# Four-layer transformer on one core: x kept in SBUF between the second layer's cross attention and its GEGLU, and the context loaded 10 slots ahead

## The chip, the core and the metric

The kernel runs on one core of a Trainium2 chip. The metric is device time in microseconds (us): the median of three runs before the change is 4973.1 us (4965.27 to 4977.62). One further execution was profiled; every view below is of that one. The engines are TensorE (PE; its weight loads are PEld), VectorE (DVE), ScalarE (ACT), GpSimd (POOL) and SyncE (SP). Each works through its own queue strictly in order. SP computes nothing: it issues the DMA transfers, and an issue at the head of its queue that has to wait holds up all behind it.

## What is computed

The input is `x`, 32 batches of 112 x 256 numbers, and a context of 32 batches of 375 x 256. Four layers follow each other; the second one is what matters here (`ln` is a layer norm, `fq` rounds to 8 bits and clips):

```python
# layer 1 (counted from 0), cut
x = attn(ln1(x), ln1(x)) + x                 # sweep l1s: self attention
x = attn(ln2(x), context) + x                # sweep l1x: cross attention, 16 heads, quantised
hg = ln3(x) @ ff_w1 + ff_b1                  # sweep l1f: GEGLU
a, g = split(hg, 2)
x = a * gelu(g) @ ff_w2 + ff_b2 + x

def attn(h, ctx):                            # 16 heads of width 16
    sim = fq(h @ wq) . fq(ctx @ wk) * scale
    out = fq(softmax(sim), dw, 0) . fq(ctx @ wv)
    return out @ wo + bo
```

Layers 0, 2 and 3 are a cross attention (l0x), a cross attention with a feed-forward (l2x, l2f), and self attention, cross attention and feed-forward (l3s, l3x, l3f). The context is the same array each time.

## The kernel before

**Sweeps, units, slots.** Each of the nine sweeps goes over all 32 batches. Two sweeps may run beside each other (`PAIRS`, L29): l1x, and with a delay l1f, are such a pair. A sweep is a list of units. A unit of l1x (`unit16`, L1005) is one batch and has 8 slots, one for each pair of heads; a unit of l1f (`unitff`, L1218) is two batches and 8 slots. `order` (L1333) merges the slots of both sweeps into one sequence by a made-up time, in which l1f runs some seven batches behind l1x.

**Work ahead of a slot.** Beside its slots a unit has atoms: pieces of work with a lead (`LEAD`, L79), the number of slots of its own sweep by which each stands ahead of the unit's first slot; a negative lead stands behind it. Atoms with cost 0 are put out when due; the others are spread as filler between slots by `fill` (L1468). `run` (L1363) writes everything out in that order, and the framework's scheduler then sets the final order of each engine's queue from a timeline of its own, and hands out the buffers. A tile names a tag; a tag has a fixed number of buffers (`BUFS`, L64), and a new tile waits until one is free.

**One pair of heads in l1x** goes through these lines: scores on PE (L1106), row maximum on DVE (L606), a small scaling on ACT (L609), the exponential on ACT (L612) into a tile of tag `k3`, times the quantisation step on ACT (L641), reciprocal on DVE (L646), scale and round on POOL or DVE (L213), clip to bf16 on DVE (L657) into another `k3` tile whose padding POOL clears (L1117). After two pairs a DMA issued by SP transposes four heads' probabilities (L1125, `k3` to `k3`), and PE multiplies them with the values (L1070). So a batch has four such transposes; I count them 0 to 3 within the batch.

**Context.** `ctx_atoms` (L530) loads one batch's context already transposed by the host (L541, 375 KB, into `k3`, then named `k<-in_ctxT_dram`), 14 slots ahead (`cload=14`). At the same lead (`cut=14`) the high part is copied into a tile of tag `k6` on ACT and DVE in turn (L200 or L202, share `("l1x", "ctx"): (1, 1, 0)`), POOL subtracts to get the low part (L231), and both are stored to DRAM (L552, `cd<-k`, 752 KB) for the later layers. The key projection on PE reads the `k6` tile first, 4 slots ahead.

**Values for layer 2.** `values_atoms` (L488) computes, as filler in l1x, four blocks a batch of layer 2's values: PE (L235 to L237), copies on ACT (first two thirds) and DVE (last third) into one `k3` tile, and a store of 375 KB (L502, `vd<-k`, 125 partitions x 3,072 bytes). So each transpose on SP has one such store near it.

**x.** In `load_x` and `store_x` (L380, L388), a sweep whose successor runs beside it can leave x in SBUF (`beside`, L373). l1x and l1f are excepted by `AGAIN` (L378): l1x loads x (lead 17) for its norm, lets the buffer go, loads x again 7 slots into the unit (`again=-7`) for the residual (L1206), and stores the sum to DRAM; l1f does the same from there (`again=-3`, residual at L832). Tag `x` has 11 buffers of 1 KB a partition, tag `k6` has 5 of 6,016 bytes.

Of the kernel before, what the change touches and what calls it, by code (L numbers as in the profile page):

```python
# [8 lines left out]
F32 = mybir.dt.float32  # L9
# [8 lines left out]
S = 112  # L18
# [3 lines left out]
D = 256  # L22
# [6 lines left out]
PAIRS = [("l0x", "l1s"), ("l1x", "l1f"), ("l2x",), ("l2f", "l3s"), ("l3x", "l3f")]  # L29
# [28 lines left out]
def mm_cost(n, m, passes):  # L58
    return passes * max(n, 2 * m) / 2.4


class Kern:
# [7 lines left out]
        l1x=[0, 1, 3, 6, 7],  # L70
        l1f=[0, 1, 5, 0, 3],
# [7 lines left out]
    LEAD = dict(  # L79
        l0x=dict(load=11, stats=10, apply=6, cload=11, cstats=8, cut=8, ctrans=5, q=4, k=[2, -2], v=-1),  # L80
        l1s=dict(load=5, stats=5, apply=3, q=2, k=2, v=1),
        l1x=dict(load=17, stats=12, apply=10, cload=14, cut=14, q=8, apart=[2, -1], k=4, v=-1, v2=[-2, -4, -6, -7], again=-7),
        l1f=dict(load=13, stats=11, apply=10, gate=2, gelu=1, again=-3),
        l2x=dict(load=10, stats=7, apply=6, cload=11, cut=7, q=4, k=[1, 1], v=0, vload=2),
        l2f=dict(load=6, stats=5, apply=3),
        l3s=dict(load=10, stats=8, apply=7, q=7, qload=3, k=6, v=3, c2=4, k2=1, v2=1),
# [285 lines left out]

    def beside(self, i):  # L373

        return any(self.sweeps[i : i + 2] == list(p) for p in PAIRS) and self.sweeps[i] not in self.AGAIN


    AGAIN = ("l1x", "l1f")  # L378

    def load_x(self, s, b):  # L380
        i = self.sweeps.index(s)
        if i and self.beside(i - 1):
            return self.xd[i - 1, b]
        x = self.t([S, D], F32, "x")
        self.nc.sync.dma_start(x, self.A["x"][b] if i == 0 else self.xd[i - 1, b])
        return x

# [440 lines left out]

    def residual(self, s, b0, g):

        for e, x in enumerate(g["xr" if s in self.AGAIN else "x"]):
            self.nc.vector.tensor_tensor(x, g["acc"][:, e, :], x, ALU.add)  # L832
            self.store_x(s, b0 + e, x)

# [170 lines left out]
    def unit16(self, s, b0, i, gb, g, wd, quant, self_attn, qb, kb, vb, dl, gvec, bvec):  # L1005
# [3 lines left out]
        L = self.LEAD[s]  # L1009
        u = Unit()  # L1010
        st = {}
        both = int(quant and self_attn)
        apart = quant and not self_attn
# [14 lines left out]
        if not self_attn and not quant and self.early_kv():  # L1028
            b = b0 + i
# [167 lines left out]
        u.slots = [quad(qd) for qd in range(4)] if self_attn else [pair(pr) for pr in range(8)]  # L1197

        def fin():
            x = st["xr"] if s in self.AGAIN else g["x"][i]  # L1200
            po = self.ps([S, D])
            wo = wd["o"]
            self.bias_mm(s, po)
            for c in range(2):
                self.mm3(po, lambda q: st["ot"][:, q, c, :], lambda q: wo[:, c, q, :], False, c == 1)
            nc.vector.tensor_tensor(x, po, x, ALU.add)  # L1206
            self.store_x(s, b0 + i, x)

        u.slots[-1].st[4] = fin
        if s in self.AGAIN:  # L1210
            u.atoms.append((L["again"], 0, lambda: st.update(xr=self.load_x(s, b0 + i))))
        return u


# [3 lines left out]
    def unitff(self, s, b0, gb, wd, gvec, bvec, b1, glu):  # L1218
        nc = self.nc
        W = gb * S  # L1220
        L = self.LEAD[s]
        u = Unit()
        u.needs = [b0 + e for e in range(gb)]
        g = {}

        u.atoms += self.norm_atoms(s, b0, gb, g, gvec, bvec, raw=glu)

        def up(ch):
            pf = self.ps([128, W])
            if glu:  # L1230
                w = wd["1", ch // 8]
                for k in range(2):
                    nc.tensor.matmul(pf, w[:, k, (ch % 8) * 128 : (ch % 8) * 128 + 128], g["h"][:, k, :], start=k == 0, stop=k == 1)  # L1233
                return pf
            w = wd["1", ch // 4]
            for k in range(2):
                self.mm3(pf, lambda i: w[:, k, i, (ch % 4) * 128 : (ch % 4) * 128 + 128], lambda i: g["h"](k, i), k == 0, k == 1)
            return pf

        def gate(c):  # L1240
            if c == 0:
                g["g"] = self.t([128, 8, W], F32, "qs")
            pf = up(c + 8)
            self.shift("gate", g["g"][:, c, :], pf, b1[:, c + 8 : c + 9])

        if glu:
            for c in range(8):
                u.atoms.append((L["gate"] + 7 - c, mm_cost(W, 0, 8), lambda c=c: gate(c)))

            u.atoms.append((L["gelu"], 0, lambda: nc.scalar.activation(g["g"], g["g"], AF.Gelu)))  # L1250

        def mk(c):
            z = {}

            def a():
                if c == 0:
                    g["acc"] = self.ps([S, gb, D], "acc")
                    self.bias_mm(s, g["acc"])
                pf = up(c)
                uu = self.t([128, W], F32, "s1")  # L1260
                if glu:
                    nc.vector.scalar_tensor_tensor(uu, pf, b1[:, c : c + 1], g["g"][:, c, :], ALU.add, ALU.mult)
                    z["uu"] = uu
                    return
                self.shift("relu", uu, pf, b1[:, c : c + 1], AF.Relu)
                ul = z["ul"] = self.t([128, 2, W], F32R, "ot")
                self.split(uu, ul[:, 0, :], ul[:, 1, :], ("upper", "lower"))

            def b():
                w = wd["2"] if glu else wd["2", c // 4]  # L1270
                for i in range(gb):
                    if glu:
                        nc.tensor.matmul(  # L1273
                            g["acc"][:, i, :], z["uu"][:, i * S : (i + 1) * S], w[:, c, :],
                            start=False, stop=c == 7 and i == gb - 1,
                        )
                        continue
                    self.mm3(
                        g["acc"][:, i, :], lambda q: z["ul"][:, q, i * S : (i + 1) * S], lambda q: w[:, c % 4, q, :],
                        False, c == 7 and i == gb - 1,  # L1280
                    )
                if c == 7:
                    self.residual(s, b0, g)

            return Slot(a, None, b)

        u.slots = [mk(c) for c in range(8)]
        if s in self.AGAIN:
            u.atoms.append((L["again"], 0, lambda: g.update(xr=[self.load_x(s, b0 + i) for i in range(gb)])))
        return u  # L1290


# [302 lines left out]
```

## Time and profile before

| | us | |
|---|---|---|
| median of three runs | 4973.1 | 4965.27 to 4977.62 |
| profiled execution | 4961.83 | its span 4960.0, so 1.8 lie around the span |
| PE busy | 4515.7 | 91% of the span |
| DVE busy | 3631.7 | 73% |
| ACT busy | 3417.2 | 69% |
| POOL busy | 2110.2 | 43% |
| l1x's score matmuls (L1106, bf16) | 1152.4 to 2309.5 | first and last start, from the span's start |

Busy time is the time in which an engine executes an instruction; waits are not in it. "PEclk" in the profile is the share of its full clock that TensorE was granted. A row of the waits names who waited, at which line and for which tile, then who ended the wait, then the total, the number and the longest. In a row of the timeline the bracket at the end is the engine's idle time just before, and what ended it.

### The profile page before, as it was taken

To read this page: it belongs to the slowest core of one execution; us is meant where nothing else is said; L and a number is where in the kernel's file an instruction comes from. 1 tells how busy PE (TensorE), PEld (TensorE's weight loads), DVE (VectorE), ACT (ScalarE), POOL (GpSimd) and SP (SyncE) were. 2 spreads that over 40 slices of the span, in tenths; PEclk is the share of its full clock that TensorE was granted. 3 is DMA by queue.
4 is the path that set the end of the run, shared out by engine and by line. 5 is a ranking of instruction groups with operands and counts; after the bars stand their busy time and mean duration, and the time that the engine had idled before them with its cause. 6 is when DMAs were issued, how large, how long until landed. Compare 5 with 4: busy or idle time off the path is not lost.

```text
span 4960.0 us, 111607 instructions
## 1 busy us (share of the span) xinstructions
PE 4515.7 (91%) x37824; PEld 4007.3 (81%) x37824; DVE 3631.7 (73%) x9806; ACT 3417.2 (69%) x10644; POOL 2110.2 (43%) x3674
## 2 busy tenths in 40 slices
PE   6999999998779888888999999998999986899999
PEld 5888888886668777777999999998888875788888
DVE  4788888888887777776688888886555554777776
ACT  4788888887777776675577777774555544677776
POOL 4455555555443333332233333334333332556655
PEclk9999999999889999999999999999999997999999
DMA  4433333335676666676454555443665666666662
GB/s 102 124 84 86 84 81 84 86 84 132 138 148 134 131 134 134 132 147 132 112 142 143 143 143 143 142 132 109 206 192 177 205 191 192 171 159 160 161 160 77
DMA packets 585414, 674.53 MB, mean 136 GB/s; under 512 B 318688, under 2 KB 495056, under 8 KB 584656
## 3 DMA queue, kind: packets, MB, share of 16 engines
q1 hardware_dynamic: 584848, 667.40, 53.3%
q8 instruction: 305, 5.00, 0.4%
q14 instruction: 261, 2.14, 0.1%
HBM read 323.55 MB, written 173.02 MB: 100 GB/s over the span
## 4 chain that ended last, share of the span: by engine, by line
PE 39%; DMA 7%; DVE 4%; ACT 1%; SPq 1%; issue 1%; POOL 1%; ACTq 0%; DVEq 0%; POOLq 0%
PE ps L664 6%; PE ps L235 5%; PE ps L236 4%; PE ps L237 4%; PE sc L773 3%; PE ps L795 3%; PE ps L1070 3%; DMA qs<-dq_l3s 2%; PE sc L1106 2%; PE acc L235 1%; PE acc L237 1%; DMA k<-cd 1%; PE acc L236 1%; PE ps L1233 1%; PE acc L1273 1%
## 5 line engine op out<-in xcount | busy, mean ns | idle before, releaser
L217 POOL TENSOR_SCALAR k<-k,sm 112x375 f32<-112x375 f32 (+1 forms) x1536 | 928.7, 617 | 1051.7 <-DVE sm L646 475.9
L200 ACT ACTIVATE k<-ps 125x336 f32<-125x336 f32 (+4 forms) x2005 | 912.4, 468 | 418.8 <-PE ps L237 194.9
L606 DVE TENSOR_REDUCE sm<-sc 112x1 f32<-112x375 f32 x1792 | 947.0, 540 | 177.0 <-PE sc L773 88.9
L612 ACT ACTIVATE k<-sc,sm 112x375 f32<-112x375 f32 x1536 | 878.2, 577 | 106.7 <-DVE sm L606 86.6
L664 PE MATMUL ps<-ident,k 112*125 112x112 f32 x4608 | 730.2, 276 | 17.4 <-issue 4.2
L664 PEld LDWEIGHTS ps<-ident,k 112*125 112x125 f32 x4608 | 649.0, 189 | 69.9 <-issue 36.3
L773 PE MATMUL sc<-k,qs 128*112 128x376 f32 x2048 | 540.9, 357 | 18.0 <-ACT k L612 9.0
L235 PE MATMUL ps<-w,k 128*125 128x256 f32 (+2 forms) x1344 | 433.4, 322 | 33.1 <-ACT k L612 17.5
L235 PE MATMUL ps<-h,w 128*128 128x224 f32 x1408 | 409.4, 297 | 42.5 <-DVE h L202 15.9
L695 DVE TENSOR_TENSOR k<-ps,k 64x376 fp32r<-64x376 f32 x640 | 350.1, 547 | 121.5 <-ACT k L200 106.2
L236 PE MATMUL ps<-h,w 128*128 128x224 f32 x1408 | 393.4, 282 | 0.5 <-DVE h L231 0.5
L202 DVE COPY k<-ps 125x336 f32<-125x336 f32 (+2 forms) x619 | 289.2, 467 | 141.2 <-PE ps L237 71.7
L237 PE MATMUL ps<-h,w 128*128 128x224 f32 x1408 | 391.5, 281 | 0.0
L236 PE MATMUL ps<-w,k 128*125 128x256 f32 (+2 forms) x1344 | 389.6, 290 | 0.0
L237 PE MATMUL ps<-w,k 128*125 128x256 f32 (+2 forms) x1344 | 388.9, 289 | 0.0
L235 PE MATMUL ps<-k,w 128*128 128x376 f32 x896 | 343.8, 384 | 41.6 <-DMA k<-cd 28.7
L213 POOL TENSOR_SCALAR k<-k,sm 112x375 f32<-112x375 f32 x256 | 164.4, 642 | 448.4 <-DVE sm L646 279.4
L795 PE MATMUL ps<-k,k 125*64 125x112 f32 (+1 forms) x4608 | 350.7, 296 | 2.1 <-ACT k L200 1.3
L773 PEld LDWEIGHTS sc<-k,qs 128*112 128x112 f32 x2048 | 304.8, 177 | 47.0 <-ACT k L612 23.6
L235 PEld LDWEIGHTS ps<-h,w 128*128 128x128 f32 x1408 | 272.3, 196 | 69.7 <-issue 20.2
L235 PEld LDWEIGHTS ps<-w,k 128*125 128x125 f32 (+2 forms) x1344 | 263.5, 196 | 73.6 <-ACT k L612 28.2
L612 ACT ACTIVATION_READ_ACCUMULATOR k<-sc,sm 112x1 f32 x1536 | 321.1, 209 | 0.0
(213 smaller groups left out, 12642.2 us busy)
## 6 DMA issues: line engine op xcount, KB each, us to landing
qs<-h SPq DMA_DIRECT2D x512, 224.0 KB
k<-k SPq DMA_DIRECT2D x192, 376.0 KB
k<-cd SPq DMA_DIRECT2D x64, 752.0 KB
vd<-k SPq DMA_DIRECT2D x128, 375.0 KB
k<-vd SPq DMA_DIRECT2D x128, 375.0 KB
qs<-dq_l3s SPq DMA_DIRECT2D x256, 112.0 KB
qs<-dq_l3x SPq DMA_DIRECT2D x256, 112.0 KB
x<-xd SPq DMA_DIRECT2D x224, 112.0 KB
```

Of the source, the lines that this page charges most:

```text
L200: self.nc.scalar.activation(out, in_, AF.Identity)
L202: self.nc.vector.tensor_copy(out, in_)
L217: self.nc.gpsimd.tensor_scalar(out, in_, by, 1.0, ALU.mult, ALU.mult)
L235: mm(out, lhs(0), rhs(0), start=start, stop=False)
L236: mm(out, lhs(0), rhs(1), start=False, stop=False)
L237: mm(out, lhs(1), rhs(0), start=False, stop=stop)
L606: nc.vector.tensor_reduce(nms[j], sc[j][:, :n], AX.X, ALU.max, negate=True)
L612: nc.scalar.activation(p[:, j, :n], sc[j][:, :n], AF.Exp, bias=nms[j], scale=1.0 if scale is None else scale, accum_out=sm[:, j : j + 1])
L664: self.nc.tensor.transpose(pst[:TB, a * S : (a + 1) * S], p[:, j, a * TB : (a + 1) * TB], self.ident[:S, :S])
L695: nc.vector.tensor_tensor(ks[o, j, :], pk[r, :TE], ks[r, j, :].bitcast(F32), ALU.subtract)
L773: nc.tensor.matmul(sc[:, :TE], qs[:, hd, q, bs], kk, start=q == 0, stop=q == 1)
L795: nc.tensor.matmul(o if gqa else o[:, mm, :], vq[:, a, hd * 64 : hd * 64 + 64], st["pt"][:, :, j, ta] if gqa else st["pt", mm][:, j, ta], ...
```

## The change

l1x and l1f no longer load x again, and l1x no longer stores x: what l1x leaves in SBUF is what l1f reads. Sixteen batches of x are held at a time: 11 in the tag `x`, and the first 5 of every 16 as slices of one tile that takes one of the five `k6` buffers from the first load of l1x until l1f's batch 20 is done. The context's load and cut move from 14 to 10 slots ahead.

```diff
-        l1x=dict(load=17, ..., cload=14, cut=14, ..., v2=[-2, -4, -6, -7], again=-7),
-        l1f=dict(load=13, stats=11, apply=10, gate=2, gelu=1, again=-3),
+        l1x=dict(load=17, ..., cload=10, cut=10, ..., v2=[-2, -4, -6, -7]),
+        l1f=dict(load=13, stats=11, apply=10, gate=2, gelu=1),
...
-        return any(self.sweeps[i : i + 2] == list(p) for p in PAIRS) and self.sweeps[i] not in self.AGAIN
-    AGAIN = ("l1x", "l1f")
+        return any(self.sweeps[i : i + 2] == list(p) for p in PAIRS)
+    ROUND, MORE = 16, 5
...
-        x = self.t([S, D], F32, "x")
+        n = b % self.ROUND
+        if s == "l1x" and n < self.MORE:
+            assert b < self.ROUND or (i + 1, b - self.ROUND) in self.xd
+            if b == 0:
+                self.more = self.t([S, self.MORE, D], F32, "k6")
+            x = self.more[:, n, :]
+        else:
+            x = self.t([S, D], F32, "x")
...
-        for e, x in enumerate(g["xr" if s in self.AGAIN else "x"]):
+        for e, x in enumerate(g["x"]):
...
-            x = st["xr"] if s in self.AGAIN else g["x"][i]
+            x = g["x"][i]
...
-        if s in self.AGAIN:
-            u.atoms.append((L["again"], 0, lambda: st.update(xr=self.load_x(s, b0 + i))))
...
-        if s in self.AGAIN:
-            u.atoms.append((L["again"], 0, lambda: g.update(xr=[self.load_x(s, b0 + i) for i in range(gb)])))
```

Lines from L385 on stand 7 further down in the changed kernel, from L1212 on 5, and from L1290 on 3. In the text both kernels' lines are named by their numbers before.

## The prediction

> **What bounds it now.** I read the header, then busy time by stretch, then the waits of the stretch that the edit touches, engine by engine, and last the timeline of one stall. By the page PE is the busiest engine:
>
> ```profile
> span 4960.0 us, 111607 instructions
> PE 4515.7 (91%) x37824; PEld 4007.3 (81%) x37824; DVE 3631.7 (73%) x9806; ACT 3417.2 (69%) x10644; POOL 2110.2 (43%) x3674
> ```
>
> The edit touches only l1x and l1f, 1150 to 2310 us. Stretches (duration, busy time and count of PE, PEld, DVE, ACT, POOL, then clock, DMA share, GB/s):
>
> ```profile
> 1000.00:1150.00 150.00, 142.89 (x1149) 120.83 (x1148) 126.50 (x366) 125.22 (x407) 81.40 (x153) 1.00 0.35 88
> 1150.00:1450.00 300.00, 231.66 (x1754) 190.55 (x1754) 266.66 (x718) 217.18 (x667) 138.24 (x252) 0.87 0.67 141
> 1450.00:2250.00 800.00, 693.71 (x5176) 614.27 (x5175) 603.96 (x1693) 564.83 (x1528) 289.25 (x444) 0.94 0.69 137
> ```
>
> Until 1450 DVE sets the pace (267 of 300 us); the edit gives it no work and takes none. From 1450 to 2250 PE is idle 106 of 800 us, and no engine is full. So that stage is bound by waits. PE's, ACT's and SP's:
>
> ```profile
> PE ps L1070 <- DMA k<-k: 64.0, 37, 5.6
> PE ps L443 <- ACT k L612: 23.1, 15, 2.5
> PE ps L235 <- ACT k L612: 9.3, 9, 2.2
> ```
>
> ```profile
> ACT k L612 <- DMA vd<-k: 22.7, 10, 4.2
> ```
>
> ```profile
> SPq L385 <- DMA xd<-x: 129.4, 42, 6.3
> SPq L502 <- DVE k L202: 129.1, 52, 8.4
> SPq L385 <- DVE xh L441: 98.7, 26, 9.1
> ```
>
> PE waits for the transposed probabilities (64 us) and for exponentials that give PSUM back. SP stands 228 us of 1160 before loads of x, which the edit removes. One stall shows the chain:
>
> ```profile
> 1637.06 0.93 SPq L541 DMA_DIRECT2D k<-in_ctxT_dram  x1
> 1639.50 0.27 SPq L502 DMA_DIRECT2D vd<-k  x1
> 1639.88 4.30 SPq L1125 DMA_TRANSPOSE k<-k  x1
> ...
> 1640.70 0.55 DVE L202 CAST k<-k 128x752 fp32r<-128x752 f32 x1 [0.35 <-DMA k<-in_ctxT_dram]
> ...
> 1647.20 0.66 ACT L612 ACTIVATE k<-ps,sm,sc 112x375 f32<-112x375 f32 x1 [4.24 <-DMA vd<-k]
> 1648.47 0.33 PE L1070 MATMUL ps<-k,k 128*32 128x112 bf16 x12 [3.66 <-DMA k<-k]
> ```
>
> The store of layer 2's values frees the buffer of the next exponential only 7 us after its issue; ACT loses 4.24 us and PE 3.66. A transpose right behind such a store takes 4.3 us to issue (42 issues within 0.3 us of one: median 4.28); from 3 us after it on, 1.5.
>
> **Removed.** 128 DMAs of 112 KB: 64 repeated loads, 32 stores by l1x, 32 first loads by l1f. Their place on the DMA engines: in 1800 to 1900 us the packets of 1,024 bytes take 90 us of 16 x 100, 6%; that lies beside other work, as the engines are busy 69%. Their SP time is what counts. I went through all 128 transposes, from the last clip (L657) to the issue: 240 us of that lateness is L385 and 50 us L396. But PE waits for 46 of them only, 79 us in all, nearly always transposes 1 and 3 of a batch, and these stand behind a value store, not behind x. Capped by PE's wait at each, the x issues cost PE 8 us. Another 20 us of lateness at the waiting ones is SP still issuing the transpose before, which x made late in part. I take **-12 us**, between -8 and -18.
>
> **Kept or added at nothing.** DVE, ACT and POOL do the same instructions on x in the same shapes. A load of x now waits for the store of the batch 16 before: in the built order 22 of 23 such loads follow that store by one to three places, some 16 pairs of waits of about 3 us (x stores landed 1.9 to 5.2 us after issue): 48 us of SP against 228. Behind it stand transposes with even number, for which PE rarely waits; uncovered it would cost those 48. With four `k6` buffers the next owner's key matmuls come at least 47 us of PE work after the last read of the old one (66 before): covered. (PE work is counted on its queue, each matmul at the 30th percentile of its form's interval from start to start, so without waits. The sum over the program is equal in both kernels, 3730 us.)
>
> **Moved: the context step.** Every batch's load, copy, subtraction and store go four slots later, 18 us at 1157 us for 256 slots, past one value store and one transpose on SP. From the load's release to the first key matmul PE had about 36 us of work, now 20. The way there: landing, copy 0.83, subtraction 1.8 with up to 2.5 of wait, some 14 us after release: covered by 5 us; if a batch used that up, PE would lose what is over.
>
> The wait that I price is the copy's. ACT and DVE reach it in order, and behind it stand the next pair's exponentials. In the built order of ACT in the changed kernel:
>
> ```
> L211 xh <- ps1
> L641, L609, L612, L612, L641
> L200 k6 <- k3        (the context's copy)
> L609, L612, L612     (next pair)
> ```
>
> Counting in PE work from the moment X at which the load may go, the instruction that feeds this copy is at X+5.5 to 6.5 before and at X+0.4 to 1.2 after, for 13 of ACT's 16 copies. After the change ACT gets there at 0.4 to 1.2 + 0.6 (L211) + 0.3 + 0.3 + 2 x 0.85 + 0.3, so about X+4.3. On SP the load now stands right behind a value store, whose last copy on DVE ends some 2 us after X: store issued at X+2.3, load at X+3.1. Alone a context load has its last packet 2.2 to 3.2 us after its issue, and is seen 0.3 later. But behind a value store? Of that the trace of before has no context load, but 13 loads of x issued within 0.7 us of one: their last packet came 3.5 to 5.8 us after issue, against a median of 1.3 for the others; value stores end 5.5 after issue. So the context lands between X+6 (unhindered) and X+8.7 (behind the store), and ACT waits 1.6 to 4.4 us. I take 4.2, the row with the same neighbour: 13 or 14 times 4.2 is 57 us of ACT.
>
> What of it reaches PE? At the ten waits of L612 for a value store (22.7 us) I summed PE's idle time during each and in the 6 us after: 26 us, of which 6 to 9 would be there anyway at 13% idle; a share of 0.75 to 1.1. I take 0.9: **+52 us** (ends: 16 from 1.6 x 14 x 0.7, and 68).
>
> DVE's 16 copies move from X+5.6 to X+3.5 to 4.2, while SP issues theirs earlier behind the transpose; DVE waits 8.6 us in 7 now. I take **+4**, between 0 and 11.
>
> **What leaves with the move.** Before, the ten L612 waits fall on pairs whose value store stood behind the context load on SP, with 2.1 to 5.3 us of PE work between the store's release and the exponential. In the built order after, the pairs of that kind have 5.9. 2.5 us more cover waits of 2.3 on average: **-20**, between -10 and -26.
>
> **Transposes.** 1 and 3 change roles: now the load stands ahead of number 3's store, afterwards near number 1's. PE work from release to use stays (15 against 20 of 126 under 6 us). No change, except that PE, held up by ACT, finds some done: **-5**, between -15 and +10.
>
> **Sum**: -12 + 52 + 4 - 20 - 5 = +19, so 4961.8 becomes 4981; the median shown is 11 above the profiled execution, so I give 4973.1 + 19, or 4992. The ends of all terms would give -43 (4930) and +71 (5044); that all meet is unlikely.
>
> The Trainium skill, "DMA: Bandwidth & Descriptors", section "Why a DMA increments its semaphore by 16 and not by 1", says that a transfer uses the largest number of engines up to 16 that divides its partitions: 5 for 125. The trace agrees: a value store's semaphore moves once at the issue and five times at the end. By its 27 GiB/s an engine the store would take an estimated 2.7 us, where the trace has 5.5; by that estimate ACT would wait about 1.5 us, and the sum would be about -14. The measurement decides. "TensorE: Matmul & The Clock Gate", Part 1, halves the clock after an idle window of about 3.4 us; the granted clock here is 0.94 against 1.00 before the stage. An estimate by it adds 1.7 us to each stall that reaches that length, at most 24 us; I leave it out.
>
> **Rivals.**
> *A, forecast: ACT waits for the context*, +19 (own range +5 to +55): 50%.
> *B, SP's relief decides*: the load lands unhindered, ACT loses 16 instead of 52, and x gives the full 18: -18 + 16 + 2 - 22 - 6 = -28, 4945. For it: 228 us of SP waits; against: PE's stalls stand behind value stores. It decides if context loads land within 3.5 us. 22%.
> *C, the exchange comes out even*: copies wait 2.5 us, PE sees 0.7 of 35 us, 25, and the rest (-12 + 4 - 20 - 5) takes 33 back: -8, 4965. 18%.
> *D, the copy's wait also reaches POOL*: the clearing of the clip's padding (L1117) already waits 26.0 us for value stores in 12 cases, and 57 instead of 42 of such waits have under 6 us in the built order. If that reaches PE too, another +35 on A: 5027. It decides if POOL's waits there pass 60 us. 10%.
> That the change does not do what it says is out: the built queue of SP has 128 DMAs fewer.
>
> **Chances.** A measurement of this kernel tells 0.3%, 15 us, from no change. A is above it in 40 of its 50, within it in 10; B below it in 20 of 22; C within it in 14, below in 4; D above in 10. Faster 24%, same 26%, slower 50%. The range reaches from B to D and a little over: 4940 to 5035; A's own is 4978 to 5028.
>
> **What would show it.** ACT's waits at L200 for the context, 4.4 us in 4 now, should be 40 to 70 in 13 or more; L612's for value stores under 8 in total; SP's at L385 under 80; L1070's 50 to 75; PE's idle time in the stage some 20 us more. The forecast is wrong if the context's copy does not wait, or if its wait does not reach PE.

## The result, and the profile after

| | before | after |
|---|---|---|
| median | 4975.36 us (6 runs, 4965.27 to 4981.68) | 5092.36 us (6 runs, 5077.47 to 5109.91) |
| ratio | 1 | 1.0224, 95% interval 1.0205 to 1.0244 |
| profiled span | 4960.0 | 5086.2 |
| l1x's score matmuls, first to last | 1152.5 to 2309.5 | 1153.7 to 2424.8 |
| PE idle and busy in that stage | 185.5 and 971.6 | 261.0 and 1010.0 |

The change makes the kernel 2.2% slower: 117 us, where 19 were forecast, and outside the range given. 114 of the span's 126 us lie in the stage that the edit touches.

In the fences of the changed kernel lines carry that kernel's own numbers: L1077 is L1070, L619 is L612, L1113 L1106, L509 L502, L392 L385, L548 L541, L559 L552, L1132 L1125; in e9, where the store takes one line more, L1078 is L1070. The header of the page:

```profile
span 5086.2 us, 111411 instructions
PE 4556.7 (90%) x37824; PEld 4036.8 (79%) x37824; DVE 3635.9 (71%) x9806; ACT 3415.8 (67%) x10644; POOL 2104.6 (41%) x3674
```

All engines but PE are busy as long as before to within 6 us; PE, with the same 37824 matmuls, 41 us longer. The stretches tell why (duration, then busy time and count of PE, PEld, DVE, ACT, POOL, then clock, DMA share, GB/s):

```profile
1150.00:1450.00 300.00, 218.78 (x1586) 182.47 (x1584) 234.88 (x651) 201.39 (x622) 124.28 (x231) 0.83 0.61 121
1450.00:2250.00 800.00, 648.58 (x4644) 562.37 (x4645) 559.15 (x1544) 507.39 (x1376) 263.39 (x406) 0.91 0.61 109
```

In 800 us PE now gets through 4644 matmuls instead of 5176, at a granted clock of 0.91 instead of 0.94. No engine has become full; there are more waits. PE's, ACT's, DVE's and SP's in the stage:

```profile
PE ps L1077 <- DMA k<-k: 99.8, 40, 7.3
PE ps L235 <- ACT k L619: 27.4, 15, 5.1
PE ps L1113 <- ACT k L619: 21.6, 17, 2.9
```

```profile
ACT k L200 <- DMA k<-in_ctxT_dram: 62.9, 14, 5.5
```

```profile
DVE k L202 <- DMA k<-in_ctxT_dram: 28.0, 11, 4.5
```

```profile
SPq L509 <- DVE k L202: 299.8, 75, 11.8
SPq L559 <- POOL k L231: 89.1, 21, 9.9
SPq L392 <- DMA xd<-x: 45.5, 12, 7.5
```

In the same stage of the kernel before the first of PE's rows and the copy's row read

```profile
PE ps L1070 <- DMA k<-k: 76.8, 45, 5.6
```

```profile
ACT k L200 <- DMA k<-in_ctxT_dram: 4.4, 4, 1.9
```

The context's copy waits as forecast (ACT 62.9 us in 14, forecast 40 to 70 in 13 or more), SP's time before x is down from 228 us to some 62, and ACT's waits for value stores went from 22.7 to 1.8. But PE's waits for transposed probabilities, forecast at 50 to 75, rose from 76.8 to 99.8, with a longest of 7.3. Two stalls show what is new. The first is the forecast one:

```profile
1597.99 0.25 SPq L509 DMA_DIRECT2D vd<-k  x1
1598.34 0.42 SPq L548 DMA_DIRECT2D k<-in_ctxT_dram  x1
...
1605.63 0.83 ACT L200 ACTIVATE k<-k 128x752 fp32r<-128x752 f32 x1 [5.11 <-DMA k<-in_ctxT_dram]
1606.54 1.78 POOL L231 TENSOR_TENSOR k<-k,k 128x752 fp32r<-128x752 f32 x1 [6.38 <-ACT k L200]
...
1607.48 0.38 PE L235 MATMUL ps<-w,k 128*125 128x256 f32 x1 [3.75 <-ACT k L619]
```

The load goes 0.35 us behind a value store and ACT gets its data 7.3 us later; ACT loses 5.11 us, POOL 6.38 and PE 3.75. The second was not foreseen:

```profile
1574.28 0.26 SPq L509 DMA_DIRECT2D vd<-k  x1
1574.63 4.24 SPq L1132 DMA_TRANSPOSE k<-k  x1
1578.98 0.70 SPq L509 DMA_DIRECT2D vd<-k  x1
...
1587.09 0.25 PE L1077 MATMUL ps<-k,k 128*32 128x112 bf16 x1 [5.89 <-DMA k<-k]
```

A transpose between two value stores, the second issued 0.1 us after it. By the trace's semaphore updates 15 of the transpose's 16 shares landed between 1581.45 and 1581.60, and the last at 1587.04, 0.03 us ahead of the store behind it. Five transposes of the changed kernel end so, and they hold 32.9 of PE's 99.8 us; none of the kernel before does. What changed is how often a transpose stands so closely, within 0.3 us, between two value stores on SP: twice before, 20 times after. Closeness alone does not decide: of the 20, five had a last share some 5 us late, four one some 1.5 us late, and eleven lost less than 1 us.

### The profile page after: what moved, and what is told of

It is laid out like the page before. It is cut to its first block, busy times and chain, and to the rows that moved or that the text cites. A ratio compares the mean times of both kernels' runs of the same rounds, so it can differ in the third digit from the quotient of the medians.

```text
span 5086.2 us, 111411 instructions
## 1 busy us (share of the span) xinstructions
PE 4556.7 (90%) x37824; PEld 4036.8 (79%) x37824; DVE 3635.9 (71%) x9806; ACT 3415.8 (67%) x10644; POOL 2104.6 (41%) x3674
## 4 chain that ended last, share of the span: by engine, by line
PE 38%; DMA 6%; DVE 4%; ACT 1%; issue 1%; SPq 1%; POOL 1%; ACTq 0%; DVEq 0%; POOLq 0%
PE ps L671 6%; PE ps L235 5%; PE ps L236 4%; PE ps L237 4%; PE ps L1077 3%; PE sc L780 3%; PE ps L802 3%; DMA qs<-dq_l3s 2%; PE sc L1113 2%; DMA k<-cd 2%; PE acc L235 1%; PE acc L237 1%; PE acc L236 1%; PE ps L1238 1%; DVE sm L613 1%
## 5 line engine op out<-in xcount | busy, mean ns | idle before, releaser
L619 ACT ACTIVATE k<-sc,sm 112x375 f32<-112x375 f32 x1536 | 878.3, 577 | 108.4 <-DVE sm L613 88.3
L619 ACT ACTIVATION_READ_ACCUMULATOR k<-sc,sm 112x1 f32 x1536 | 321.1, 209 | 0.0
```

The lines of the kernel that those rows point to most:

```text
L619: nc.scalar.activation(p[:, j, :n], sc[j][:, :n], AF.Exp, bias=nms[j], scale=1.0 if scale is None else scale, accum_out=sm[:, j : j + 1])
```

## The experiments

The theory after the result: the value store (375 KB, 125 partitions) holds up whatever shares its way, and the new lead puts the context's load behind it. Rivals: x in SBUF itself (four `k6` buffers, loads behind stores); the mere distance of 10 slots; SP's in-order waits. Each ratio below is against the kernel before on the same chip. "Copies" are ACT's and DVE's waits for the context together, "A·V" PE's waits for transposed probabilities, "late shares" the transposes whose last share landed 2.7 us or more after the middle one.

| run | ratio (95%) | median | PE idle, busy in the stage | copies | A·V | late shares |
|---|---|---|---|---|---|---|
| before | 1 | 4975 | 186, 972 | 13 | 77 | 0 |
| after | 1.0224 | 5092 | 261, 1010 | 91 | 100 | 5 |
| e1 x in SBUF, lead 14 | 0.9956 (0.9934 to 0.9977) | 4968 | 174, 981 | 4 | 69 | 1 |
| e2 x loaded again, lead 10 | 1.0198 (1.0171 to 1.0226) | 5080 | 269, 1011 | 86 | 105 | 2 |
| e3 before, four `k6` | 1.0003 (0.9990 to 1.0017) | 4984 | 197, 971 | 15 | 79 | 1 |
| e4 load 14, copy 10 | 0.9980 (0.9960 to 1.0000) | 4972 | 179, 980 | 1 | 69 | 0 |
| e5 lead 9 | 1.0059 (1.0038 to 1.0081) | 5011 | 222, 991 | 23 | 96 | 3 |
| e6 lead 11 | 1.0154 (1.0121 to 1.0188) | 5056 | 250, 1004 | 4 | 137 | 6 |
| e7 lead 8 | 1.0234 (1.0203 to 1.0264) | 5101 | 269, 1021 | 107 | 77 | 2 |
| e8 store on POOL's queue | 1.0188 (1.0162 to 1.0214) | 5076 | 262, 1007 | 93 | 103 | 7 |
| e9 after, stores in two | 0.9841 (0.9810 to 0.9871) | 4899 | 136, 957 | 40 | 1 | 0 |
| e10 lead 14, stores in two | 0.9790 (0.9769 to 0.9811) | 4879 | 120, 941 | 4 | 3 | 0 |
| e11 lead 11, stores in two | 0.9816 (0.9791 to 0.9842) | 4893 | 125, 956 | 2 | 8 | 0 |
| e12 before, stores in two | 0.9775 (0.9754 to 0.9796) | 4871 | 122, 943 | 5 | 4 | 0 |
| e13 after, third store in two | 1.0069 (1.0044 to 1.0093) | 5018 | 212, 988 | 46 | 81 | 4 |
| e14 after, the others in two | 1.0002 (0.9986 to 1.0019) | 4982 | 179, 975 | 85 | 14 | 0 |
| e15 after, stores 115 + 10 | 1.0077 (1.0049 to 1.0104) | 5022 | 220, 993 | 78 | 57 | 5 |
| e16 before, all in two | 0.9586 (0.9563 to 0.9608) | 4776 | 118, 951 | 3 | 7 | 0 |
| e17 before, other stores in two | 0.9826 (0.9804 to 0.9847) | 4901 | 134, 948 | 5 | 24 | 0 |
| e18 before, third store in two | 0.9963 (0.9947 to 0.9978) | 4967 | 178, 980 | 5 | 57 | 0 |

**Which half of the change costs.** e1 and e4 edit the changed kernel, e2 the one before; e3 is the kernel before with an idle tile in one of the five `k6` buffers.

```diff
e1  -cload=10, cut=10   +cload=14, cut=14
e2  -cload=14, cut=14   +cload=10, cut=10
e4  -cload=10, cut=10   +cload=14, cut=10
e3  +if s == "l1x" and b == 0:
    +    self.held = self.t([128, 2, 2, TE], F32R, "k6")
    +    self.nc.gpsimd.memset(self.held[:, 0, 0, 0:8].bitcast(F32), 0.0)
    +if s == "l1f" and b == 20:
    ...
    +    self.nc.gpsimd.tensor_copy(sink, self.held[:, 0, 0, 0:2].bitcast(F32))
```

> The changed kernel with only the lead put back: x stays in SBUF, the context is loaded and copied 14 slots ahead as before. Theory L (the later context is the whole loss, and x in SBUF is a small gain): 4950 to 4980 us, ACT's wait at L200 for the context under 10 us. Theory K (four k6 buffers, or the new wait of the x loads for stores, carry the loss): above 5040 us, with waits of ACT or DVE for a k6 buffer or of SP for x stores.

> The kernel before with only the lead changed from 14 to 10; x is loaded again as before and k6 keeps five buffers. Theory L: 5080 to 5120 us, the whole loss and the x issues besides; ACT's wait at L200 above 40 us. Theory K: 4980 to 5000 us.

> The kernel before, lead 14, x loaded again, but one of the five k6 buffers is held by an idle tile for as long as the changed kernel holds it (the only extra work is one small memset and two small copies on POOL). Theory L: within 0.3% of before, 4960 to 4990 us, since the next owner's key matmuls have 47 us of PE work or more. Theory K: above 5020 us.

> The changed kernel with the context loaded 14 slots ahead but copied and stored 10 ahead, so that the data has landed long before the copy; one more k3 buffer of eleven is held for some 18 us a batch. Theory L1 (the copy's wait for a transfer in flight is the cause): ACT's and DVE's waits at L200 and L202 for the context under 5 us, time 4950 to 4990. Theory L2 (the later place of copy, subtraction and store is the cause, whatever the load does, since SP stands at the store until POOL has subtracted): above 5050. Theory L3 (the k3 buffer held longer costs): also above 5000, with new waits of ACT at L619 and of POOL at L1124 for k3 buffers.

The lead is the whole loss: x in SBUF alone is 22 us faster, lead 10 alone 2.0% slower, four buffers cost nothing that can be told. In e4 copy, subtraction and store stand as late as in the changed kernel and nothing is lost; so it is the load's own place that costs, not the later place of what follows it.

**Distance or neighbour.** In the built order leads 8 and 10 put most loads right behind the third value store of a batch; 9, 11 and 14 put them ahead of a store. e5 to e7 change only the numbers; e8 issues the context's store from POOL.

```diff
e5  +cload=9, cut=9
e6  +cload=11, cut=11
e7  +cload=8, cut=8
e8  -nc.sync.dma_start(d.bitcast(F32), o.bitcast(F32))
    +nc.gpsimd.dma_start(d.bitcast(F32), o.bitcast(F32))
```

> The changed kernel with the context one slot later still, 9 instead of 10. In its built order of SP 29 of the 32 context loads stand behind a transpose and ahead of a value store; at 10, 17 of 32 stand directly behind a value store. Theory N (the neighbour on SP decides: a load right behind a value store lands late): 4955 to 5000 us, loads landed within 3 us of their issue, ACT's wait at L200 for the context under 15 us. Theory D (the distance decides, less lead is worse): 5090 us or more, ACT's wait at L200 above 60.

> The changed kernel with the context 11 slots ahead. In the built order 28 of the 32 loads stand behind a transpose, 24 of them ahead of a value store, none right behind one. Theory N: 4950 to 4990 us. Theory D: 5040 to 5080, between lead 10 and lead 14.

> The changed kernel with the context 8 slots ahead; in the built order 23 or more of the 32 loads stand right behind a value store again. Theory N: 5070 to 5140 us, as many late loads as at 10 or more, and ACT's wait at L200 60 to 90 us. Theory D: above 5100. Together with leads 9 and 11 a saw-tooth is for N, a slope for D.

> The changed kernel at lead 10, with the store of the context's two parts issued from POOL's queue and not from SP's; SP's order is otherwise the same. POOL does the subtraction before the store, so there the store waits for nothing. Theory S (SP's 89 us before this store, while POOL waits for the late copy, are what makes the late loads cost so much: value stores and transposes behind it go out late and close together): 5000 to 5045 us, and at most one transpose whose last share lands 3 us or more after the others. Theory C (ACT, DVE and POOL carry the late copy to PE by themselves): 5070 to 5100 us. The issue itself costs POOL some time, of which no run here shows the size.

Distance is out: 9 is faster than 10 and than 11 (though 11 us above what theory N allowed). The neighbour explains the copies: the 18 loads of the changed kernel within 0.5 us behind a store have their last packet 6.45 us after the end of the issue (median), its other 14 after 2.67, the 32 of before after 2.43; 26 stand so at lead 8, none at 9 and 11. The semaphores show how. In each of those 18 loads eleven of the 16 shares landed 2.3 to 3.6 us after the issue, and the other five after 5.8 to 7.7, about 1 us behind the five landing steps of the store ahead. (At lead 8 ACT's copies wait 54 us, where theory N gave 60 to 90, and DVE's 53.) But it does not explain lead 11, which by that theory should have taken 4950 to 4990; its 5056 lies where theory D had it. There hardly a copy waits, and PE's waits for transposes are the longest of all (1150 to 2410 us):

```profile
PE ps L1077 <- DMA k<-k: 138.2, 55, 7.6
```

```profile
ACT k L200 <- DMA k<-in_ctxT_dram: 0.9, 1, 0.9
```

The six transposes with a late share hold 39 us of it. So there is a second loss, and the next runs ask whether the same store makes it. e8 takes SP's 89 us before the context's store away and comes to 1.0188, whose interval overlaps that of 1.0224, with seven late shares where theory S gave one at most: theory S is out, that wait was covered.

**The store itself.** From here the value store goes out in two DMAs; e13, e14, e17 and e18 do that for some of the four stores of a batch only.

```diff
-                    self.nc.sync.dma_start(d, z["v"])
+                    self.nc.sync.dma_start(d[:112], z["v"][:112])
+                    self.nc.sync.dma_start(d[112:], z["v"][112:])
```

> The changed kernel (lead 10) with each value store issued as two: partitions 0 to 111 and 112 to 124. SP's order is otherwise the same, 18 of 32 context loads still stand right behind a store. Theory M (the one store's five landing steps are the cause: everything with a share behind them ends with it, the context after 6.5 us instead of 2.4, and the last share of a transpose that stands between two stores 5 us late): context loads land within 4 us also behind a store, ACT's wait at L200 falls from 63 to under 25 us, no transpose has a share 2.7 us or more late, time 4930 to 4985. Theory O (the order that the scheduler writes for this lead, and SP's in-order waits, are the cause): 5070 us or more, with 128 more issues on SP.

> x in SBUF with lead 14, and the value store in two parts as in the run at lead 10. Theory M: 4900 to 4955 us, below the same kernel with one store (4968), since transposes behind a store land sooner and ACT's wait at L612 for value stores (30 us there) goes. Theory O: 4965 to 4990, the same or slower for the added issues.

> x in SBUF with lead 11, and the value store in two parts. With one store this lead had no late context load and still lost 1.5%, with 138 us of PE's waits at the transposed probabilities, six of them for a last share. Theory M: the six go and the time falls to 4910 to 4975, within 20 us of lead 14. Theory O: 5040 us or more.

> The kernel before with the value store in two parts, nothing else. Theory M: 4920 to 4970 us; with it the whole change (x in SBUF and lead 10, both with the split) should be worth between -30 and +15 us and not +117. Theory O: 4975 to 5010.

Theory M, and all four below the times that it gave; but ACT's wait in e9, 32 us, stayed above its 25, and the change costs 33 us where it gave 15 at most. The whole store's semaphore moves once at the issue and five times at the end, the last 5.9 us (before) or 6.2 us (after) after the end of the issue; the parts of 112 and 13 move theirs 16 and 14 times and land after 3.0 and 2.9. In e9 a load right behind a store has its last packet after 3.52 us, and the two waits read

```profile
PE ps L1078 <- DMA k<-k: 0.8, 2, 0.6
```

```profile
ACT k L200 <- DMA k<-in_ctxT_dram: 32.2, 13, 3.0
```

99 us of PE's waits for transposes are gone, and half of the copy's. The late shares are only a third of those 99: a transpose right behind a whole store took SP 4.3 us to issue and had landed 8.2 us after the start of its issue (medians of the changed kernel; 4.3 and 7.3 before), and in e9 1.8 and 4.1. The three leads 10, 11 and 14 now lie within 0.51%, and the change costs 0.66%, 33 us. Its first half, 22 us better with the store whole, is now worth nothing that can be told (0.9790 against 0.9775, intervals overlap).

> The changed kernel (lead 10), with only the third of a batch's four value stores in two parts, the one beside which the context load stands. Theory Q (the two losses are separate): context loads land within 4 us, ACT's wait at L200 is 25 to 40 us as with all stores split, so 51 us of ACT and DVE waits go at about 0.8; the transposes beside the other three stores stay late, PE's waits at the transposed probabilities 60 to 95 us; time 4990 to 5040. Theory R (the late copy is the root, and the transposes are only late because of it): 4900 to 4960, with under 50 us of PE's waits there.

> The changed kernel with the other three stores in two parts, and the one beside the context load whole. Theory Q: ACT's wait at L200 stays 50 to 75 us, PE's waits at the transposed probabilities fall to 10 to 45 us; time 4930 to 4990. Theory R: 5040 us or more.

> The kernel before with the first, second and fourth value store of a batch in two parts and the third whole: the pair of the run that does the same to the changed kernel (4982 us). What the change costs there is the late copy's part. Theory Q (copy and transposes are two separate parts): the copy's 72 us more of ACT and DVE waits at 0.8 to 1.1, so 58 to 80 us, and this run at 4902 to 4924. Theory R (the copy carries nearly all): 100 us or more, 4882 or less.

> The kernel before with only the third value store of a batch in two parts: the pair of the changed kernel with the same (5018 us). What the change costs there is the transposes' part and half of the copy's. Theory Q: 55 to 85 us, this run at 4933 to 4963. Theory R: 20 to 45 us, 4973 or more.

e13 and e14 came out as theory Q gave (5018 and 4982 us, A·V 81 and 14), and far from theory R. With e17 and e18 they make a square that divides the loss, by differences of ratios times 4980 us. With all stores in two the change costs 33 us (0.66%). With only the third whole, which stands beside the load, 88 (1.0002 less 0.9826); with only the others whole, 53 (1.0069 less 0.9963); with all whole, 112. So the whole store beside the load adds 55 to the 33 and the others 20; 33 + 55 + 20 is 108 of 112. By the intervals of the runs the 55 and the 20 are sure to some 23 us either way: the 55 is clear of zero, the 20 and an interaction are not. That the transposes have a part of their own is seen in PE's waits for them, which go when the other stores are cut (14 us in e14) and stay when the third is (81 in e13). e17 and e18 came 1 us under and 4 us over what theory Q gave; the differences of 88 and 53 lie outside its 58 to 80 and 55 to 85, and outside theory R's too.

> The changed kernel with every value store in two parts of 115 and 10 partitions: as many issues as with 112 and 13, but 115 has no divisor up to 16 but 5 either. Theory E (the number of landing steps of the large part matters): the large store lands after 4.5 us or more, context loads behind it after 5.5 or more, time 5050 to 5110. Theory F (a store in two parts is better whatever the parts are): below 4950 us.

Neither. The part of 115 moves its semaphore six times, as 125 does, and lands after 5.38 us, loads behind it after 5.34, near what theory E gave for both: for the landing the number of parts is not what matters. But the time fell by 1.5%, where E expected next to nothing, and A·V by 42 us. Besides the landing, 0.8 to 1.1 us earlier, a transpose right behind a store took SP 3.05 us to issue and not 4.35, and the late shares were some 3 us late and not 5; which of these brought the 1.5% this run does not separate.

> The kernel before with every transfer of 125 partitions in parts of 112 and 13: the value stores of l1x, the loads of them in l2x, the context's load in l0x, and the stores and loads of values in l3s and l3x. The value stores alone gave 4871 us. Theory G (such transfers hold up their neighbours wherever there are many): 4780 to 4850. Theory H (only l1x has waits that stand behind them): 4860 to 4890.

The best version, 4.1% faster than before, and below what theory G gave. All transfers of 125 partitions go through one helper:

```diff
+    def parts(self, o, i):
+        self.nc.sync.dma_start(o[:112], i[:112])
+        self.nc.sync.dma_start(o[112:], i[112:])
-                    self.nc.sync.dma_start(d, z["v"])
+                    self.parts(d, z["v"])
...
-            nc.sync.dma_start(kv["v"], self.vd[b0 + i, qd])
+            self.parts(kv["v"], self.vd[b0 + i, qd])
...
```

From e12 to e16 the stage stays (1065 and 1069 us), and 90 of the 97 us of span are won behind it (2650 to 2560 us), where most of these transfers are; which of them won it no run separates.

```profile
span 4768.8 us, 112422 instructions
PE 4455.6 (93%) x37824; PEld 3956.8 (83%) x37824; DVE 3620.9 (76%) x9806; ACT 3412.7 (72%) x10644; POOL 2107.8 (44%) x3674
```

## Why the prediction was wrong

The direction and the place were right, the size was not: 19 us were forecast, 117 measured. The runs split the miss. The lead alone (e2) costs 99 us, between 85 and 112, where its terms (+52, +4, -20, -5) add up to +31; x alone at this lead gives nothing that can be told, where -12 was taken. Two steps failed. "Transposes: no change" missed that PE's waits for them would rise (99.8 us in place of 50 to 75). The credits of -12 and -20 counted waits that did go as time saved, and by the account below little or none came. By its own steps:

- **Copy on ACT, 57 us of wait in 13 or 14.** Right: 62.9 in 14. The price came from x loads behind a store; the context behaves like them, only later (6.45 us after the issue, against 5.6 taken).
- **Copy on DVE, +4 (0 to 11).** Too small: 8.6 became 28.0. Counting places in the built order gave DVE's loads as earlier; on the chip five of them, too, went right behind a store.
- **Share that reaches PE, 0.9.** Fair, as far as differences between runs that also differ otherwise can tell: between e10 and e9 36 us more of waits cost 25 (0.7), between e17 and e14 80 more cost 88 (1.1). With DVE's part the copies waited 78 us more than before; at these shares their term is an estimated +55 to +86, where +56 was taken.
- **Transposes, -5 (-15 to +10).** This step failed. I took no change because PE's work between release and use stays the same, and left out the neighbourhood: 20 transposes and not 2 now stand closely between two stores, five of them give PE their last share 5 us late, and PE's waits rose from 76.8 to 99.8 us. By the square this part is +20, sure to some 23 either way.
- **Credits of -12 (x) and -20 (L612).** This step failed too. Both waits went, as said, but the time did not come. x in SBUF is worth 22 us at lead 14 (e1) and nothing that can be told at lead 10 (1.0224 with it, 1.0198 without). What L612's waits were worth by themselves no run here separates. With +55 to +86 and +20 for copies and transposes, 112 leave an estimated +6 to +37 for all else, where -32 was taken: by this account it is the largest miss of the sum.
- **Clock, left out.** It should have been in. PE's busy time in the stage rose 38 us for the same 7260 matmuls. After the 5.89 us stall above the granted clock (the column behind POOL's) stood at 0.50 for 3 us and at a mean of 0.78 for 3 more:

```profile
1587.00:1590.00 3.00, 2.91 (x19) 1.99 (x18) 1.34 (x7) 1.65 (x5) 0.47 (x1) 0.50 0.31 68
1590.00:1593.00 3.00, 3.00 (x20) 2.87 (x19) 1.45 (x5) 2.61 (x5) 0.35 (x1) 0.78 0.00 0
```

  By the trace's clock records it was halved from 1584.5 to 1591.3 us and full again after. In the whole stage it was halved for 174 us before and for 273 after. If PE lost half of its time at half clock, the 99 us more would bring at most some 50; 38 were measured. PE's stalls of 3.4 us or more went from 9 to 20, but shorter ones count as well: in the kernel before a stall of 2.46 us that ended at 1980.70 was followed by a granted clock of 0.51 until 1984.20.
- **Four `k6` buffers and loads of x behind stores at nothing.** Right (e3, e1). In the whole stage before, though, stores of x landed 1.8 to 8.7 us after their issue, not 1.9 to 5.2.
- **Rival D**, POOL's waits at L1117 past 60 us: they reached 38, so it did not decide. No rival named the late share.

The Trainium skill, "DMA: Bandwidth & Descriptors", section "Why a DMA increments its semaphore by 16 and not by 1", which the prediction used for the store's landing steps, also gives the numbers on which the cure rests: by its rule 112 partitions go over 16 engines, 13 over 13, 115 over 5 and 10 over 10, and the semaphores agree (16, 14, 6 and 11 moves, the issue's own counted where there is one). "TensorE: Matmul & The Clock Gate", Part 1, halves the clock after an idle window of some 3.4 us; the 0.50 above agrees, the 0.51 after 2.46 us shows that shorter stalls do it here too. An estimate by the page, 1.7 us for each of 11 more stalls of that length, is 19 us, half of the 38 measured.

**What stays open:** why six transposes end late at lead 11 and three at lead 9, although 22 and 24 stand closely between two stores; why lead 11 still loses more than these six hold; what part of the gain of cutting the store comes from its earlier landing and what part from the shorter issue of the transposes behind it; and the 33 us that the change costs with stores in two, of which the copies' remaining 40 us of waits are the likely, not the shown, cause.

## What to carry to other kernels

Before tuning leads, look at how many steps each DMA's semaphore takes to land: a transfer of 125 partitions in five steps held up loads and transposes around it, and cutting it into 112 and 13 was worth 2.3%, all of them 4.1%, while of the 2.2% that the change studied here cost all but 0.66% went once these stores were cut. A moved load is priced by what stands next to it on its queue after the move, read from the built order, and so are the transfers that it pushes together. A wait of several microseconds on PE's path can cost more than itself: in this stage 76 us more of idle time came with 38 us more of busy time for the same matmuls, at a mean granted clock that fell from 0.92 to 0.89.

## What the runs showed of the hardware that was not expected

- A transpose of 16 shares delivered 15 within 0.15 us, and the last with a value store issued 0.1 us after it, 5.5 us later (1587.04 against 1581.60); seen only where a store followed within 1.6 us of the transpose, not each time (five of the 20 of the changed kernel that stand within 0.3 us between two stores), and never where all stores went in parts of 112 and 13; in parts of 115 and 10 five were some 3 us late.
- A 375 KB load alone had its last packet after 2.4 us, and after 6.45 right behind a whole value store, 3.5 behind one in parts of 112 and 13, though its first packet came 0.6 to 0.8 us after the issue in all three. Behind the whole store exactly five of its 16 shares were late, as many as the store's landing steps.
- In parts of 115 and 10 (e15) the store landed 0.8 us earlier and 42 of 100 us of PE's waits for transposes were gone.
- The 32 stores of the context issued by POOL (e8) added 25 us to POOL's busy time (2130.1 against 2104.6); each issue took POOL 0.64 us, and SP 0.35 us in the changed kernel (medians).
